# An audio layer on one core: joint index masks, a third index tile, and attention's output computed transposed

## The chip, the core and the metric

The kernel runs on one core of a Trainium2 chip. A core has five engines with queues of their own: PE (TensorE, matmuls from SBUF into PSUM; its weight loads are shown as PEld), DVE (VectorE), ACT (ScalarE), POOL (GpSimd) and SP (SyncE, which here issues every DMA). Each engine runs its own instructions in the order in which the program holds them, and waits where a semaphore says so. The metric is the device time of one execution in microseconds, lower being better.

## The reference

32 recordings of 160,000 samples are cut into S = 313 frames of 512 samples and transformed by a cosine basis. One layer follows: layer norm, attention with eight heads (softmax times a decay matrix, a group norm per head, a gate), a residual; then layer norm, a feed-forward part and a residual.

```python
h = einsum('bfh,kh->bfk', frames, D)
# attention, X = layernorm(h)
Q, K = xpos(X @ W_Q), xpos(X @ W_K, downscale)
p = softmax(Q @ K.T) * gamma ** abs(n - m)
Y = p @ V
Yn = (Yg - mu) * rsqrt(var + 1e-5)          # by head
h = h + (silu(X @ W_G) * (Yn * gn_weight + gn_bias)) @ W_O
# feed-forward, x = layernorm(h)
theta = x[..., None, :] / (1 + abs(W)) + B_param     # 256 units x 512 features
idx = mod(round(theta * 4096 / 2pi), 4096)
c, s = sum(cos_t[idx] * attn_cos, -1), sum(sin_t[idx] * attn_sin, -1)
h = h + silu(c @ proj_cos.T + s @ proj_sin.T)
```

The feed-forward part carries the bulk of the work: for each of 32 x 313 frames, 256 units and 512 features, one sine and one cosine.

## The kernel before, in words

**Feed-forward.** The 512 features lie as 4 groups of 128 partitions, frames along the free axis. Sequences go in pairs. A round handles 32 of the 256 units for the pairs that are resident just then (one to four of them, r = 2 to 8 sequences), so a pair stays for eight rounds; `STARTS` says in which of the 42 rounds each of the 16 pairs joins. There are 4 rounds of one pair, then 6 of two, 4 of three, 22 of four, and 2 each of three, two and one at the end. A round's work is cut into slots of at most 16 x 313 elements (two, four or eight combinations of a unit and a feature group; 12 x 313 elements with three pairs). For each slot:

- DVE writes table indices as int16 into a tile `ix` (L610, one instruction for each combination and run of neighbouring pairs), masks them in place (L622), writes a copy shifted by a quarter period into the next tile (L630) and masks that one in place (L636).
- ACT takes a sine of each of the two tiles into tiles `trig` (L643, "sines").
- PE multiplies each piece of `trig` by 32 columns of `hot`, which hold the attention weights of one unit in one column, and so adds up over features (L664, `pa` in PSUM). At the end of a round DVE copies the sums out (L681) and SP stores them.

Four `ix` tiles, three `trig` tiles, two `hot` tiles (one for each two units, 256 KB) and two tiles `f` (scale and offset of a round's units) rotate.

**Attention** of one sequence is laid between the slots. 313 rows are three blocks of 105 that overlap by one row. The buffers are in `Buffers`: three `ring` tiles through which all weights come, two `dec` tiles for decay matrices, `h`, `xn`, `xnT`, `prob`, `probT`, `u`, and four PSUM banks `W`. Two sequences are done before the first round (buffers A and B side by side), the other 30 with A during rounds. Its steps, in order: transform (`rows`, L273), layer norm (statistics L236, inverse root by `rsqrt`, normalisation L248), transposes (L260), values, and for each group of heads queries, keys and their rotated copies (`columns`, L288), the rotation in three DVE products (L341 to L346), scores (L355), maximum and difference (L363, L372), exponentials on ACT, row sums (L397), and for each head transposes (L412), the product with the decay (L424), the product with the values (L430: probabilities as stationary operand, result in rows) and the copy of it (L443). The group norm squares and sums (L467, L472 to L477), takes an inverse root, scales (L484), transposes back, and applies weight and bias (L494) and the gate (L499). `output` makes the last projection of a sequence (L531, L534).

`rsqrt` is two DVE instructions that make a seed (L215, L218) and twelve POOL instructions, three Newton steps of four (L224 to L227).

**What sets the order.** `Plan` takes every step with a key (its due place), an engine, an estimated duration, and what it reads and writes. `emit` runs a list schedule on these estimates: an engine that is free takes, of the steps whose predecessors have ended (plus `WAIT`, 400 ns, and for a load `LAND`, 3,500 ns), the one with the lowest key. The order found is the order in each engine's queue, SP's included. The estimates decide nothing else: on the chip an engine waits for what it really needs.

Of the kernel before, what the change touches and what calls it, by code (L numbers as in the profile page):

```python
# [21 lines left out]
P = 128  # L22
# [104 lines left out]
def tile_audio_tower(ctx: ExitStack, tc: tile.TileContext, t: dict, out: bass.AP):  # L127
# [7 lines left out]
    N_RING = 3  # L135
    N_IX, N_TRIG, N_HOT, N_PA = 4, 3, 2, 4
# [15 lines left out]
    class Buffers:  # L152


        def __init__(self, name, pool, psum):
            self.name = name
            self.n_ring = 0

# [4 lines left out]
            self.dec = [sb(f"dec{i}", STEP * (NT - 1) + S) for i in range(2)]  # L163

            self.u = sb("u", NC4, S)
            self.qk = [self.u[:, 2 * i : 2 * i + 2, :] for i in range(2)]
            self.h = sb("h", NT, HOP)
            self.v = self.h
            self.xn = sb("xn", NT, HOP)
            self.xnT = sb("xnT", NC4, S)  # L170
            self.prob = sb("prob", NB, NT, S)
            self.probT = sb("probT", NT, S)
            self.raw = self.probT[:, 0:2, :]
            wide = self.prob.rearrange("p a b s -> p (a b s)")
            self.sq = wide[:, : NT * HOP].rearrange("p (i d) -> p i d", d=HOP)
            self.hres = self.sq
            self.aff = wide[:, NT * HOP : NT * HOP + NC4 * S].rearrange("p (c s) -> p c s", s=S)
# [8 lines left out]

            self.y = self.W[:, 3, : NT * 2 * DH].rearrange("p (i d) -> p i d", d=2 * DH)
# [24 lines left out]
    def rsqrt(plan, key, val, r, u, kv, kr, ku):  # L212
# [17 lines left out]
        plan.add(key, "POOL", 3500, newton, (kv,), (kr, ku))  # L230

    def layernorm(plan, key, x):

        for i in range(NT):
            def stats(i=i):
                nc.vector.bn_stats(x.st[:N, i, :], x.h[:N, i, :])  # L236
                nc.vector.bn_aggr(x.mv[:N, i, :], x.st[:N, i, :])
            plan.add(key, "DVE", 850, stats, (x.k("h"),), (x.k("mv", i),))
# [6 lines left out]
        for i in range(NT):  # L245
            plan.add(
                key, "DVE", 490,
                lambda i=i: nc.vector.tensor_scalar(  # L248
                    x.xn[:N, i, :], x.h[:N, i, :], x.mv[:N, i, 0:1], x.lr[:N, i : i + 1],
                    ALU.subtract, ALU.mult,  # L250
                ),
                (x.k("h"), x.k("mv", i), x.k("lr")), (x.k("xn", i),),
            )

    def transposed(plan, key, x):

        for c in range(NC4):
            def go(c=c):
                for i in range(NT):
                    nc.tensor.transpose(  # L260
                        x.W[:, c, ROW0[i] : ROW0[i] + N], x.xn[:N, i, c * P : (c + 1) * P],
                        ident[:N, :N],
                    )
            plan.add(key, "PE", 800, go, x.every("xn", NT), x.banks(c))
# [28 lines left out]
    def attention(plan, keys, sq, x, eng):  # L293
# [9 lines left out]
        def residual(key, load):  # L303
            for i in range(NT):
                f0 = 1 if i and not load else 0
                d, s = h_d[sq, ROW0[i] + f0 : ROW0[i] + N, :], x.h[f0:N, i, :]
                kd, ks = ("h_d", sq), x.k("h")
                if load:
                    plan.add(key, "SP", DMA_NS, lambda d=d, s=s: nc.sync.dma_start(s, d), (kd,), (ks,))
                else:  # L310
                    plan.add(key, "SP", DMA_NS, lambda d=d, s=s: nc.sync.dma_start(d, s), (ks,), (kd,))

        xns, probs, us = x.every("xn", NT), x.every("prob", NB), x.every("u", 2)
# [3 lines left out]
        copy(plan, step(), eng, NT * HOP, x.h[:N], W3, x.banks(0, 1, 2), (x.k("h"),))  # L317
# [8 lines left out]
        copy(plan, step(), eng, NT * HOP, x.v[:N], W3, x.banks(0, 1, 2), (x.k("h"),))  # L326
        plan.add(step(0), "POOL", 500, lambda: nc.gpsimd.memset(x.v[0:1, : NT - 1, :], 0.0), (),
                 (x.k("h"),))

        for hb in range(H // NB):  # L330
            for g in range(hb * NB // 2, (hb + 1) * NB // 2):
# [8 lines left out]
                plan.add(key, "DVE", 810,  # L340
                         lambda qk=qk: nc.vector.tensor_tensor(qk, x.W[:, 0:2, :S], cos_qk, ALU.mult),  # L341
                         x.banks(0, 1), (kq,))

                def turned(qk=qk):
                    nc.vector.tensor_tensor(x.raw, x.W[:, 2:4, :S], sin_qk, ALU.mult)
                    nc.vector.tensor_tensor(qk, qk, x.raw, ALU.add)  # L346
                plan.add(key, "DVE", 1640, turned, x.banks(2, 3), (x.k("probT"), kq))
            for hd in range(hb * NB, (hb + 1) * NB):
# [16 lines left out]
                if a == NB - 1:  # L365
# [9 lines left out]
                         (x.k("mx", hd % 2), *x.banks(0, 1, 2)), (x.k("prob", a),))  # L375

            def exps(hb=hb, m=m):
                if eng == "DVE":
                    nc.scalar.activation(x.prob[:N, : NB - 1], x.prob[:N, : NB - 1], AF.Exp)
                for a in range(NB):  # L380
                    for i in range(NT):
                        last = a == NB - 1
                        if last or eng == "ACT":
                            nc.scalar.activation(  # L384
                                x.prob[:N, a, i, :],
                                x.W[:N, i, :S] if last else x.prob[:N, a, i, :], AF.Exp,
# [7 lines left out]
                     (x.k("mx", 1), *x.banks(0, 1, 2)), [*probs, x.k("sm", hb), x.k("lu")])  # L394
            for a in range(0, NB if eng == "DVE" else 0, 2):
                plan.add(step(0), "DVE", 2120,
                         lambda h0=hb * NB + a, a=a: nc.vector.tensor_reduce(  # L397
                             x.sm[:N, :, h0 : h0 + 2].rearrange("p i h -> p h i"),
                             x.prob[:N, a : a + 2], AX.X, ALU.add),
                         (x.k("prob", a), x.k("prob", a + 1)), (x.k("sm", hb),))  # L400
            for hd in range(hb * NB, (hb + 1) * NB):
                key = step(5)
                a, d = hd % NB, hd % 2
                plan.add(key, "SP", DMA_NS,
                         lambda hd=hd, d=d: nc.sync.dma_start(x.dec[d], t["decay"][hd]),
                         (), (x.k("dec", d),))
                for jj in range(NT):
                    j = NT - 1 - jj

                    def go(a=a, jj=jj, j=j):  # L410
                        for i in range(NT):
                            nc.tensor.transpose(  # L412
                                x.W[:N, jj, ROW0[i] : ROW0[i] + N],
                                x.prob[:N, a, i, ROW0[j] : ROW0[j] + N], ident[:N, :N],
                            )
                    plan.add(key, "PE", 800, go, (x.k("prob", a),), x.banks(jj))

                def decayed(d=d):
# [535 lines left out]
```

## Time and profile before

| What | us |
|---|---|
| median of three runs (18,890.79 to 18,904.49) | 18,893.47 |
| the profiled execution | 18,894.1 |
| its span, first to last instruction | 18,892.3 |
| ACT busy in sines, 4,288 of them (L643) | 17,547.6 |
| DVE busy in indices (L610), 5,888 instructions | 6,673.8 |
| DVE busy in L622, L630 and L636, 2,144 each | 3,023.7, 3,014.4, 3,017.3 |
| PE busy in the sine matmuls (L664), 131,072 | 10,373.1 |
| PE busy in the value products (L430), 4,464 for buffers A | 540.6 |
| POOL busy in all | 656.5 |

A busy time is a sum over one kind of instruction on one engine, and the engines work beside each other, so the rows do not add up to the span. PE's share says little by itself, since its matmuls are pipelined and their ends are modelled. What a row is worth is seen from the stage it lies in and from what the other engines wait for there.

### The profile page before, as it was taken

To read this page: it belongs to the slowest core of one execution; us is meant where nothing else is said; L and a number is where in the kernel's file an instruction comes from. 1 tells how busy PE (TensorE), PEld (TensorE's weight loads), DVE (VectorE), ACT (ScalarE), POOL (GpSimd) and SP (SyncE) were. 2 spreads that over 40 slices of the span, in tenths; PEclk is the share of its full clock that TensorE was granted. 3 is DMA by queue.
4 is the path that set the end of the run, shared out by engine and by line. 5 is a ranking of instruction groups with operands and counts; after the bars stand their busy time and mean duration, and the time that the engine had idled before them with its cause. 6 is when DMAs were issued, how large, how long until landed. Compare 5 with 4: busy or idle time off the path is not lost.

```text
span 18892.3 us, 332980 instructions
## 1 busy us (share of the span) xinstructions
PE 14803.3 (78%) x148864; PEld 6590.0 (35%) x148864; DVE 17770.2 (94%) x15244; ACT 18090.3 (96%) x5026; POOL 656.5 (3%) x1222
## 2 busy tenths in 40 slices
PE   8888888887888887888788888887888788766566
PEld 4433333333333333333333333333333333222222
DVE  5999999999999999999999999999999999889998
ACT  3899999999999999999999999999999999999998
POOL 0000000000000000000000000000000000000000
PEclk8999999999999999999999999999999999889998
DMA  3211111111111111111111111111111111000011
GB/s 96 66 52 48 50 57 47 46 51 47 31 35 37 46 42 41 32 40 46 38 45 39 32 44 41 45 40 36 39 38 46 39 45 35 24 10 25 12 30 46
DMA packets 447834, 783.69 MB, mean 41 GB/s; under 512 B 61601, under 2 KB 116129, under 8 KB 446401
## 3 DMA queue, kind: packets, MB, share of 16 engines
q1 hardware_dynamic: 446400, 762.39, 13.3%
q8 instruction: 1167, 19.12, 0.4%
q14 instruction: 267, 2.18, 0.0%
HBM read 657.51 MB, written 104.66 MB: 40 GB/s over the span
## 4 chain that ended last, share of the span: by engine, by line
DVE 55%; ACT 18%; PE 15%; issue 8%; POOL 3%; DMA 1%; DVEq 0%; SPq 0%; ACTq 0%; POOLq 0%
DVE ix L610 20%; ACT trig L643 18%; DVE ix L630 9%; DVE ix L622 9%; PE pa L664 8%; DVE ix L636 8%; PE a_W L288 3%; PE a_W L273 2%; DVE a_mx L363 1%; DVE a_prob L372 1%; DVE a_sm L397 1%; DVE a_probT L424 1%; DVE a_st L236 1%; PE a_W L355 1%; POOL a_lu L224 1%
## 5 line engine op out<-in xcount | busy, mean ns | idle before, releaser
L643 ACT ACTIVATE trig<-ix 128x5008 f32<-128x5008 int16 (+1 forms) x4288 | 17547.6, 4178 | 442.0 <-PE pa L664 185.5
L664 PE MATMUL pa<-trig,hot 128*32 128x313 f32 x131072 | 10373.1, 462 | 3021.0 <-ACT trig L643 3003.0
L664 PEld LDWEIGHTS pa<-trig,hot 128*32 128x32 f32 x131072 | 4058.5, 116 | 8907.0 <-ACT trig L643 4513.9
L610 DVE TENSOR_SCALAR ix<-xT,f 128x2504 int16<-128x2504 f32 (+3 forms) x5888 | 6673.8, 1184 | 211.9 <-ACT trig L643 205.8
L630 DVE TENSOR_SCALAR ix<-ix 128x5008 int16<-128x5008 int16 (+1 forms) x2144 | 3014.4, 1406 | 201.2 <-DVE ix L622 5.0
L622 DVE TENSOR_SCALAR ix<-ix 128x5008 int16<-128x5008 int16 (+1 forms) x2144 | 3023.7, 1410 | 69.2
L636 DVE TENSOR_SCALAR ix<-ix 128x5008 int16<-128x5008 int16 (+1 forms) x2144 | 3017.3, 1407 | 67.2
L288 PE MATMUL a_W<-a_xnT,a_ring 128*128 128x313 f32 x4960 | 1539.2, 446 | 220.1 <-DVE a_u L341 125.1
L273 PE MATMUL a_W<-a_ring,a_u 128*105 128x512 f32 x2256 | 1101.5, 623 | 120.8 <-DVE a_u L499 53.7
L288 PEld LDWEIGHTS a_W<-a_xnT,a_ring 128*128 128x128 f32 x4960 | 882.9, 191 | 868.2 <-issue 284.7
L430 PE MATMUL a_W<-a_h,a_probT 105*105 105x64 f32 x4464 | 540.6, 270 | 118.0 <-DVE a_probT L424 117.7
L273 PEld LDWEIGHTS a_W<-a_ring,a_u 128*105 128x105 f32 x2256 | 360.2, 174 | 722.8 <-issue 579.0
L430 PEld LDWEIGHTS a_W<-a_h,a_probT 105*105 105x105 f32 x4464 | 476.3, 181 | 386.4 <-issue 194.7
L355 PE MATMUL a_W<-a_u 64*105 64x313 f32 x1488 | 502.8, 466 | 112.0 <-DVE a_prob L372 100.6
L412 PE MATMUL a_W<-ident,a_prob 105*105 105x105 f32 x2232 | 325.9, 284 | 186.7 <-ACT a_prob L384 150.9
L273 PE MATMUL a_W<-a_ring,a_xnT 128*105 128x512 f32 x744 | 380.0, 631 | 50.9 <-DVE a_xnT L210 49.3
L224 POOL TENSOR_TENSOR a_gu<-a_gr 105x24 f32<-105x24 f32 x93 | 69.5, 747 | 10066.3 <-DVE a_gr L218 10061.4
L412 PEld LDWEIGHTS a_W<-ident,a_prob 105*105 105x105 f32 x2232 | 259.4, 185 | 344.9 <-ACT a_prob L384 193.2
L260 PE MATMUL a_W<-ident,a_xn 105*128 105x105 f32 x1116 | 190.2, 298 | 234.8 <-DVE a_xn L248 108.2
L355 PEld LDWEIGHTS a_W<-a_u 64*105 64x105 f32 x1488 | 239.3, 178 | 386.0 <-DVE a_prob L372 152.6
L363 DVE TENSOR_REDUCE a_mx<-a_W 105x3 f32<-105x939 f32 x248 | 280.2, 1130 | 17.7 <-PE a_W L355 17.1
L424 DVE TENSOR_TENSOR a_probT<-a_W,a_dec 105x939 f32<-105x939 f32 x248 | 279.9, 1129 | 13.0 <-PE a_W L412 13.0
(136 smaller groups left out, 3461.9 us busy)
## 6 DMA issues: line engine op xcount, KB each, us to landing
hot<-in_hot SPq DMA_DIRECT2D x672, 256.0 KB
a_dec<-in_decay SPq DMA_DIRECT2D x248, 260.5 KB
a_ring<-in_proj SPq DMA_DIRECT2D x128, 256.0 KB
a_ring<-in_dct SPq DMA_DIRECT2D x124, 256.0 KB
a_ring<-wv_d SPq DMA_DIRECT2D x124, 256.0 KB
a_ring<-in_wq SPq DMA_DIRECT2D x124, 256.0 KB
a_ring<-in_wk SPq DMA_DIRECT2D x124, 256.0 KB
a_ring<-in_wq_s SPq DMA_DIRECT2D x124, 256.0 KB
```

The costliest lines, as they stand in the source:

```text
L273: lambda c=c, i=i, k=k, to=to: nc.tensor.matmul(x.W[:N, to, :], lhsT[:, c, ROW0[i] : ROW0[i] + N], x.ring[k], start=(c == 0), stop=(c == N ...
L288: lambda c=c: nc.tensor.matmul(x.W[:, bank, :S], w[:, c, :], x.xnT[:, c, :], start=(c == 0), stop=(c == NC4 - 1)),
L355: lambda i=i, qk=qk, r0=r0: nc.tensor.matmul(x.W[:N, i, :S], qk[r0 : r0 + DH, 0, ROW0[i] : ROW0[i] + N], qk[r0 : r0 + DH, 1, :], start=Tru ...
L363: lambda m=m: nc.vector.tensor_reduce(m[:N], x.W[:N, :NT, :S], AX.X, ALU.max),
L412: nc.tensor.transpose(x.W[:N, jj, ROW0[i] : ROW0[i] + N], x.prob[:N, a, i, ROW0[j] : ROW0[j] + N], ident[:N, :N],)
L430: nc.tensor.matmul(x.y[:N, i, (hd % 2) * DH : (hd % 2 + 1) * DH], x.probT[:N, jj, ROW0[i] : ROW0[i] + N], x.v[:N, jj, hd * DH : (hd + 1) * ...
L610: nc.vector.tensor_scalar(now["ix", x][:, d0 : d0 + 2 * m * S], now["xT", c][:, 2 * at * S : 2 * (at + m) * S], f[:, 0, c, n + u : n + u + ...
L622: nc.vector.tensor_scalar(tl, tl, LUT - 1, LUT // 2, ALU.bitwise_and, ALU.bitwise_xor)
L630: nc.vector.tensor_scalar(tl[:, :E], now["ix", xs][:, :E], float(LUT // 4), None, ALU.add)
L636: nc.vector.tensor_scalar(tl, tl, LUT - 1, None, ALU.bitwise_and)
L643: nc.scalar.activation(tl[:, :E], now["ix", x][:, :E], AF.Sin, bias=-PI32, scale=ANG)
L664: nc.tensor.matmul(now["pa", p][g * 32 : g * 32 + 32, :S], now["hot", z][:, u, c, k, :], now["trig", w][:, s0 : s0 + S], start=(n == 0 and ...
```

## The change

- **Joint masks.** A tile `ix` now holds two halves. Indices go into the first half, one instruction writes the quarter-shifted copy into the second, and one instruction masks both. There are three such tiles in place of four single ones. Slots, sines and sine matmuls are as many as before.
- **Hot tiles** are cut in half (two units by two feature groups, 128 KB) and there are three of them. Tiles `f` go from two to one, `ring` from three to two, `dec` from two to one.
- **Values as stationary operand.** A value block of 105 x 64 is the weight, the transposed probabilities stream through, and the result comes out with features on partitions (`yT`). Heads are taken in the order 3, 2, 0, 1 of each four.
- **Group norm** on that layout: squares, sums over the 64 features of a head by matmuls with a matrix of ones (`of_head`), two fused instructions for the variance, the inverse root as before, three transposes of the 24 factors, a copy, and matmuls with `head_w`, which holds the weights, to spread the factors over the features; one product and four fused additions of the bias and products with the gate. The transposes back are gone.
- **The rotation** is one product over all four banks and one addition. Row sums are taken over one and over three heads instead of two and two. The layer norm writes its result over `h`; tile `xn` is gone.
- The planner's estimate for Newton's steps on POOL is 6,000 in place of 3,500, and estimates of the changed DVE steps are set anew.

```diff
-    N_RING = 3
-    N_IX, N_TRIG, N_HOT, N_PA = 4, 3, 2, 4
+    N_RING = 2
+    N_IX, N_TRIG, N_HOT, N_PA = 3, 3, 3, 4
...
-            self.dec = [sb(f"dec{i}", STEP * (NT - 1) + S) for i in range(2)]
+            self.dec = sb("dec", STEP * (NT - 1) + S)
...
-        plan.add(key, "POOL", 3500, newton, (kv,), (kr, ku))
+        plan.add(key, "POOL", 6000, newton, (kv,), (kr, ku))
...
-                for i in range(NT):
-                    def go(i=i, hd=hd):
-                        for jj in range(NT):
-                            nc.tensor.matmul(
-                                x.y[:N, i, (hd % 2) * DH : (hd % 2 + 1) * DH],
-                                x.probT[:N, jj, ROW0[i] : ROW0[i] + N],
-                                x.v[:N, jj, hd * DH : (hd + 1) * DH],
-                                start=(jj == 0), stop=(jj == NT - 1),
-                            )
-                    plan.add(key, "PE", 1000, go, (x.k("probT"), x.k("h")), x.banks(3))
+                e0 = hd % 2 * DH
+                for jj in range(NT):
+                    plan.add(
+                        key, "PE", 500,
+                        lambda jj=jj, hd=hd, e0=e0: nc.tensor.matmul(
+                            x.W[e0 : e0 + DH, 3, :S], x.v[:N, jj, hd // 2, e0 : e0 + DH],
+                            x.probT[:N, jj, :], start=(jj == 0), stop=(jj == NT - 1)),
+                        (x.k("probT"), hs[hd // 2]), x.banks(3))
...
+        def sums():
+            for i in range(NT):
+                for c in range(NC4):
+                    nc.tensor.matmul(x.W[:N, 0, i * H : (i + 1) * H],
+                                     x.sqT[:, c, ROW0[i] : ROW0[i] + N], of_head[:, c, :],
+                                     start=(c == 0), stop=(c == NC4 - 1))
+        plan.add(key, "PE", 2700, sums, probs, x.banks(0))
...
+            nc.vector.scalar_tensor_tensor(f(x.gv), f(x.sm), EPS, f(x.sm), ALU.mult, ALU.mult)
+            nc.vector.scalar_tensor_tensor(
+                f(x.gv), x.W[:N, 0, : NT * H], 1.0 / DH, f(x.gv), ALU.mult, ALU.add)
...
+        def factors():
+            for i in range(NT):
+                nc.tensor.transpose(x.W[:H, 1, ROW0[i] : ROW0[i] + N], x.gr[:N, i, :], ident[:N, :N])
+        plan.add(step(2), "PE", 700, factors, (x.k("gr"),), x.banks(1))
...
+        def spread():
+            for c in range(NC4):
+                nc.tensor.matmul(x.W[:, c, :S], head_w[:, c, :], x.rT, start=True, stop=True)
...
-                        def mask(x=x):
-                            tl = now["ix", x][:, :E]
-                            nc.vector.tensor_scalar(
-                                tl, tl, LUT - 1, LUT // 2, ALU.bitwise_and, ALU.bitwise_xor)
-                        plan.add(key, "DVE", 130 + 0.26 * E, mask, (), (("ix", x),))
...
-                        def quarter(x=x, xs=xs):
-                            tl = new("ix", x, [P, SLOT * S], I16, bufs=N_IX)
-                            nc.vector.tensor_scalar(
-                                tl[:, :E], now["ix", xs][:, :E], float(LUT // 4), None, ALU.add)
...
-                        def wrap(x=x):
-                            tl = now["ix", x][:, :E]
-                            nc.vector.tensor_scalar(tl, tl, LUT - 1, None, ALU.bitwise_and)
...
+            def quarter(x=x, E=E):
+                tl = now["ix", x]
+                nc.vector.tensor_scalar(tl[:, 1, :E], tl[:, 0, :E], float(LUT // 4), None, ALU.add)
+            plan.add(key, "DVE", 220 + 0.26 * E, quarter, (("ix", x, 0),), (("ix", x, 1),))
+
+            def mask(x=x, E=E):
+                tl = now["ix", x][:, :, :E]
+                nc.vector.tensor_scalar(
+                    tl, tl, LUT - 1, LUT // 2, ALU.bitwise_and, ALU.bitwise_xor)
+            plan.add(key, "DVE", 220 + 0.26 * 2 * E, mask, (), [("ix", x, i) for i in range(2)])
```

## The prediction

> **What bounds the kernel now.** I read the page's busy shares first, then busy time by stage, then the instruction groups by shape, then the waits, and last a timeline of one stall. The profiled execution took 18,894.1 us (span 18,892.3), 0.003% above the median of the runs shown, so sums made on it carry over.
>
> ```profile
> PE 14803.3 (78%) x148864; PEld 6590.0 (35%) x148864; DVE 17770.2 (94%) x15244; ACT 18090.3 (96%) x5026; POOL 656.5 (3%) x1222
> ```
>
> ScalarE is idle for 802 us in all, so a change that leaves its work alone can win no more than that. The columns of the next view are window, length, then busy us and (instructions) of PE, PEld, DVE, ACT, POOL.
>
> ```profile
> 0.00:331.00 331.00, 279.13 (x1088) 181.54 (x1088) 137.92 (x186) 52.60 (x122) 17.77 (x82) 0.85 0.37 115
> 331.00:1020.00 689.00, 559.10 (x5051) 282.33 (x5052) 647.79 (x852) 593.84 (x246) 37.59 (x76) 0.89 0.22 66
> 1020.00:2840.00 1820.00, 1481.63 (x14401) 689.85 (x14403) 1743.48 (x1688) 1705.04 (x490) 82.43 (x152) 0.93 0.17 51
> 2840.00:4690.00 1850.00, 1490.20 (x14578) 673.65 (x14574) 1763.55 (x1654) 1730.82 (x577) 77.78 (x152) 0.96 0.15 47
> 4690.00:16060.00 11370.00, 9176.72 (x92958) 4075.45 (x92950) 10878.04 (x8237) 11243.61 (x2879) 440.89 (x760) 0.93 0.13 40
> 16060.00:18892.00 2832.00, 1816.48 (x20812) 687.14 (x20804) 2599.46 (x2632) 2764.43 (x716) 0.00 (x0) 0.91 0.08 24
> ```
>
> Length minus ACT's column gives ACT's idle time: 278 us before the first sine, then 95, 115 and 119 in the rounds of one, two and three pairs ("early", 329 in 4,359 us), 126 in the wide rounds with attention, 68 at the end. Early, VectorE is the busier engine (4,155 against 4,030); wide, ScalarE is (98.9%). So DVE work taken out counts early, and little later.
>
> ```profile
> ACT trig L643 <- PE pa L664: 52.2, 25, 3.8
> ACT trig L643 <- DVE ix L636: 29.9, 29, 2.5
> ACT a_xn L531 <- PE a_W L273: 20.2, 9, 3.8
> ...
> ACT trig L643 <- DVE ix L622: 7.0, 11, 3.9
> ```
>
> These are ACT's waits in the wide rounds (4,690 to 16,060; total us, times, longest): only 37 of its 126 idle us are charged to DVE.
>
> **The joint mask.** Of a slot's five or more DVE instructions it removes one: mask, quarter and wrap become a quarter and one mask over both halves.
>
> ```profile
> L622 DVE TENSOR_SCALAR ix<-ix 128x5008 int16<-128x5008 int16 x1760 | 2586.2, 1469 | 57.5
> L622 DVE TENSOR_SCALAR ix<-ix 128x3756 int16<-128x3756 int16 x384 | 437.6, 1139 | 11.7
> ```
>
> The two shapes give (1,469 - 1,139) / 1,252 = 0.26 ns an element and a fixed part near 0.166 us (all three lines agree within 5 ns). The elements stay, so each slot saves one fixed part: 2,144 slots x 0.166 = 356 us of DVE, of which 512 slots (64 + 192 + 256) lie early: **85 us**. [...] A gap of some 31 ns before the dropped instruction (69.2 us over 2,144) may go too: 0 to 16 us early, taken as 8. Where three pairs run, the joint mask is a pattern of 2 x 3,756, a shape the trace lacks. Its bounds are 2.1 us (this rate) and 4.1 us (half of it); I take the first, because element type and step are those of the row.
>
> **Attention on DVE, per sequence**: the rotation, four times 0.804 + 0.806 + 0.812, becomes 1.46 (a 1,252-element row) + 0.812, -0.6; four output copies at 0.551 become 0.478 (the 128x313 copy from PSUM), -0.3; squares 1.755 to 1.46, -0.3; variance 1.747 + 0.293 + 0.183 + 0.183 + 0.178 becomes two of 0.18, -2.2; the 1.758 scaling becomes a 0.478 copy and a 1.46 product, +0.2; the affine part, 4 x 0.596 + 1.46, becomes four fused ones whose price lies between 0.478 and 0.596, taken as 0.55, -1.6. Row sums keep their elements. Sum -4.9 us; ten sequences finish early: **49 us**. ScalarE loses only five squares of about 0.3 us.
>
> **PE** nets nothing. 144 narrow y matmuls, 540.6 / 31 = 17.4 us a sequence, become 48 wide ones at 0.31 (1,539 / 4,960), 14.9. Twelve transposes go (2.0); 24 tiny matmuls with ones (0.121 each, 2.9), three transposes (0.5) and 8 spreading matmuls (2.5) come: +1.4 us.
>
> **Newton on POOL** is planned at 6.0 us instead of 3.5, so DVE is given more work before it asks for the result. Now it waits 2.4 us each time (below: total, times, longest), 67 us of this early, with the 2.3 us waits at L484.
>
> ```profile
> DVE a_xn L248 <- POOL a_lr L227: 150.4, 62, 3.3
> ```
>
> Would the longer plan remove that? Here is one such stall.
>
> ```profile
> 7484.79 1.39 POOL L224 TENSOR_TENSOR a_lu<-a_lr 105x3 f32<-105x3 f32 x1 [77.72 <-DVE a_lr L218]
> 7486.26 1.42 POOL L225 TENSOR_TENSOR a_lu<-a_lu,a_lv 105x3 f32<-105x3 f32 x1
> 7487.76 1.41 POOL L226 TENSOR_SCALAR a_lu<-a_lu 105x3 f32<-105x3 f32 x1
> 7489.26 0.19 POOL L227 TENSOR_TENSOR a_lr<-a_lr,a_lu 105x3 f32<-105x3 f32 x1
> ```
> ```profile
> 7484.55 3.07 DVE L610 TENSOR_SCALAR ix<-xT,f 128x2504 int16<-128x2504 f32 x2
> 7487.66 1.47 DVE L622 TENSOR_SCALAR ix<-ix 128x5008 int16<-128x5008 int16 x1
> 7491.69 1.46 DVE L248 TENSOR_SCALAR a_xn<-a_h,a_mv,a_lr 105x512 f32<-105x512 f32 x3 [2.57 <-POOL a_lr L227]
> ```
>
> Three POOL operations end just after three DVE instructions; once DVE stands still they take 0.19 us, one every 0.275. [...] By the plan's figure alone all 67 us would go. [...] Net **9 us**. [...]
>
> **Loads.** Ring buffers go from 3 to 2, decay from 2 to 1, the scale table f from 2 to 1, hot tiles from two whole to three halves. These loads now wait for a nearer reader: f for the last index of its round, decay for the previous head's product, hot for PE two halves back. A sums load landed 2.1 us after its issue, and f is covered by the 4.2 us of quarter and mask, so 0 if SP is free; if SP, which issues in order, stands at a hot load, DVE waits up to 3 us a round, 14 early rounds, 0 to 42. I take 5. In one-pair rounds a slot needs two of the three hot halves; freeing one, issue and landing (0.4 + 2.1) and the 2.3 us run that follows make about 5 us, under the slot's 8.56, so 0, and 64 early slots x 1 us if a load is held. Before the first sine the two sequences alternate on PE (279 of 331 us busy): cheaper y, a longer group-norm chain and thinner rings: -15 to +15, taken as 0. The last two outputs reload two ring tiles late, +3; the 32 last slots of one pair give 5 back.
>
> **Sum.** Early DVE: 85 + 8 + 49 + 9 - 5 = 146, leaving DVE at 4,213 against ACT's 4,030, so still the bound; I let nine tenths through, 131, since part of ACT's early idle time (58.1 + 29.7 + 39.9 = 128 us) is charged to PE, which gains nothing. Wide: a third joint index tile lets DVE run three slots ahead instead of two and its load falls; the 37 us go. End: 2. Total 170: 18,894 - 170 = 18,724, **forecast 18,720**, own range 18,650 to 18,800.
>
> **Rivals.**
> - *Everything couples* (0.2): early ACT idles only as in the wide rounds, 1.1% of 4,359 = 47, so 282 go, and with it half of the wide 126: 18,550. For it: ACT's own early work allows it. Against: the DVE sum has only 146.
> - *PE takes the wait* (0.14): the 128 us charged to PE stay and the thinner loads eat the wide gain; 60 are won: 18,830. For it: attention's bursts of 10.5 us on PE block sines now. Against: DVE never starved for it long.
> - *The factors block PE* (0.05), the slower side: group-norm factors reach PE only when POOL is done. [...] Three sine tiles cover 3 x 4.28 less two runs of 2.3, 8.2 us. From there each microsecond is ACT's. If PE stands 15 us, 7 x 30 = 210 are lost and 170 won: 18,935.
> - *The joint mask doesn't do what it says* (0.01): at half rate 2.5 us a slot, DVE bound throughout: above 20,000.
>
> The forecast keeps 0.6. The range reaches to both near rivals and the bounds of loads and start: 18,560 to 18,850. Under 0.2% (38 us) a measurement of this kernel would not tell a change. Faster 0.87: forecast, coupling and most of the PE case; same 0.07; slower 0.06.
>
> **What would show it.** A joint mask at 2.77 us and 2.1; DVE busy down by about 510 us and ACT unchanged; the early stages shorter by some 130 us, ending near 4,560; waits of the normalisation on POOL at 1.6 us instead of 2.4; no new wait on f or hot. I am wrong if the early end hardly moves, if ACT's waits on PE grow around the factors, or if the wide rounds gain more than 60.

## The result and the profile after

The changed kernel takes 18,708.7 us (median of 4 runs, 18,703.5 to 18,713.1) where the kernel before takes 18,895.2 on the same chip: a ratio of 0.9900 (95% interval 0.9886 to 0.9914). That is 186 us less, against 170 to 174 forecast. The profiled execution has a span of 18,701.4 us, 191 less than before.

The sum came out nearly right, its parts did not. The stages, cut at the sines that begin them, show it; the last two columns are ACT's idle time.

| Stage | before, us | after, us | difference | expected | idle before | idle after |
|---|---|---|---|---|---|---|
| before the first sine | 331.0 | 356.8 | +26 | 0 | 278 | 304 |
| rounds of one pair | 697.3 | 705.3 | +8 | about -20 | 98 | 106 |
| rounds of two pairs | 1,828.7 | 1,778.7 | -50 | about -55 | 113 | 66 |
| rounds of three pairs | 1,837.7 | 1,779.3 | -58 | about -55 | 119 | 64 |
| rounds of four pairs ("wide") | 12,476.2 | 12,363.1 | -113 | -37 | 134 | 29 |
| the rest | 1,721.4 | 1,718.2 | -3 | -2 | 60 | 61 |

("About" is the forecast's 131 us of the early stages, spread over them.) The first line of the changed kernel's page, the busy time by engine, stands against the one shown of before:

```profile
PE 14815.8 (79%) x146528; PEld 6384.0 (34%) x146528; DVE 17294.6 (92%) x12876; ACT 18071.2 (97%) x5026; POOL 1038.5 (6%) x1190
```

DVE has lost 476 us of work, ACT 19, and POOL is busy 1.6 times as long with fewer instructions. By window (columns as before: window, length, then busy us and instructions of PE, PEld, DVE, ACT, POOL):

```profile
356.80:1062.20 705.40, 582.87 (x4939) 275.46 (x4940) 633.74 (x781) 599.06 (x248) 51.93 (x74) 0.89 0.22 65
1062.20:2840.90 1778.70, 1494.17 (x14196) 670.88 (x14199) 1707.86 (x1476) 1712.94 (x492) 136.75 (x148) 0.93 0.18 53
2840.90:4620.20 1779.30, 1483.35 (x14224) 648.86 (x14217) 1700.05 (x1363) 1715.55 (x576) 141.87 (x148) 0.95 0.16 48
4620.20:16983.20 12363.00, 9900.25 (x99725) 4222.56 (x99723) 11546.06 (x7351) 12333.62 (x3136) 689.54 (x740) 0.93 0.13 38
```

With two and three pairs ACT is now a little busier than DVE, where it was the other way round: DVE no longer bounds these stages by its work. With one pair DVE is busier still, and DVE stands idle for 72 and ACT for 106 of 705 us, so something else holds them. In the wide rounds ACT is busy for 99.8% of the window. Its waits there, from 4,625 us on (total us, times, longest; the stage's first wait, 7.4 us for the joint mask, lies before):

```profile
ACT trig L651 <- DVE ix L643: 14.1, 10, 3.0
ACT trig L651 <- PE pa L673: 5.8, 8, 0.9
ACT trig L651 <- issue: 4.9, 2, 2.5
ACT a_h L550 <- PE a_W L278: 1.8, 1, 1.8
```

(L651 is the sines, L643 the joint mask, L673 the sine matmuls, L278 the row products, L550 the output's activation.) Not only the waits charged to DVE are gone, as forecast: of those charged to PE, 54.0 us in the sines and 25.9 in the output over the whole wide stage, 7.6 are left. That is the second thing to explain; the first is the beginning, where 34 us were lost and 20 should have been won.

### The profile page after: what moved, and what is told of

Its sections match the earlier page's. It is cut to its first block, busy times and chain, and to the rows that moved or that the text cites. A ratio compares the mean times of both kernels' runs of the same rounds, so it can differ in the third digit from the quotient of the medians.

```text
span 18701.4 us, 327934 instructions
## 1 busy us (share of the span) xinstructions
PE 14815.8 (79%) x146528; PEld 6384.0 (34%) x146528; DVE 17294.6 (92%) x12876; ACT 18071.2 (97%) x5026; POOL 1038.5 (6%) x1190
## 2 busy tenths in 40 slices
DMA packets 716481, 783.43 MB, mean 42 GB/s; under 512 B 72344, under 2 KB 470936, under 8 KB 715072
## 3 DMA queue, kind: packets, MB, share of 16 engines
q1 hardware_dynamic: 715072, 762.46, 13.6%
## 5 line engine op out<-in xcount | busy, mean ns | idle before, releaser
L651 ACT ACTIVATE trig<-ix 128x5008 f32<-128x5008 int16 (+1 forms) x4288 | 17531.7, 4177 | 278.3 <-PE pa L673 143.3
L673 PE MATMUL pa<-trig,hot 128*32 128x313 f32 x131072 | 10330.4, 460 | 3243.6 <-ACT trig L651 3184.5
L673 PEld LDWEIGHTS pa<-trig,hot 128*32 128x32 f32 x131072 | 4053.3, 115 | 9223.5 <-ACT trig L651 4911.7
L626 DVE TENSOR_SCALAR ix<-xT,f 128x2504 int16<-128x2504 f32 (+3 forms) x5888 | 6657.8, 1182 | 87.9 <-DMA xT<-xT_d 62.5
L643 DVE TENSOR_SCALAR ix<-ix 128x10016 int16<-128x10016 int16 (+1 forms) x2144 | 5686.4, 2652 | 65.0
L638 DVE TENSOR_SCALAR ix<-ix 128x5008 int16<-128x5008 int16 (+1 forms) x2144 | 3028.7, 1413 | 633.8 <-ACT trig L651 479.6
L278 PE MATMUL a_W<-a_ring,a_u 128*105 128x512 f32 x2256 | 1098.8, 620 | 73.7 <-DMA a_u<-in_frames 23.9
L229 POOL TENSOR_TENSOR a_gu<-a_gr 105x24 f32<-105x24 f32 x93 | 101.5, 1092 | 9975.8 <-DVE a_gr L223 9776.0
L278 PEld LDWEIGHTS a_W<-a_ring,a_u 128*105 128x105 f32 x2256 | 358.1, 174 | 674.6 <-issue 618.4
L445 PE MATMUL a_W<-a_probT,a_h 105*64 105x313 f32 x1488 | 494.1, 464 | 43.6 <-DVE a_probT L438 43.4
L278 PE MATMUL a_W<-a_ring,a_xnT 128*105 128x512 f32 x744 | 367.1, 619 | 11.4 <-DVE a_xnT L215 9.9
L229 POOL TENSOR_TENSOR a_lu<-a_lr 105x3 f32<-105x3 f32 x186 | 149.2, 802 | 3587.4 <-DVE a_lr L223 3577.6
L445 PEld LDWEIGHTS a_W<-a_probT,a_h 105*64 105x64 f32 x1488 | 192.8, 147 | 358.5 <-issue 159.1
L426 PE MATMUL a_W<-ident,a_prob 105*105 105x105 f32 x1674 | 244.8, 275 | 11.4 <-DVE a_h L455 11.3
L426 PEld LDWEIGHTS a_W<-ident,a_prob 105*105 105x105 f32 x1674 | 183.5, 172 | 187.8 <-issue 158.6
L347 DVE TENSOR_TENSOR a_prob<-a_W,turn_qk 128x1252 f32<-128x1252 f32 x124 | 180.4, 1454 | 66.7 <-issue 35.2
```

Source lines behind the costliest of these rows:

```text
L278: lambda c=c, i=i, k=k, to=to: nc.tensor.matmul(x.W[:N, to, :], lhsT[:, c, ROW0[i] : ROW0[i] + N], x.ring[k], start=(c == 0), stop=(c == N ...
L426: nc.tensor.transpose(x.W[:N, jj, ROW0[i] : ROW0[i] + N], x.exp[a][:N, i, ROW0[j] : ROW0[j] + N], ident[:N, :N],)
L445: lambda jj=jj, hd=hd, e0=e0: nc.tensor.matmul(x.W[e0 : e0 + DH, 3, :S], x.v[:N, jj, hd // 2, e0 : e0 + DH], x.probT[:N, jj, :], start=(jj ...
L626: nc.vector.tensor_scalar(now["ix", x][:, 0, d0 : d0 + 2 * m * S], now["xT", c][:, 2 * at * S : 2 * (at + m) * S], f[:, 0, c, n : n + 1], ...
L638: nc.vector.tensor_scalar(tl[:, 1, :E], tl[:, 0, :E], float(LUT // 4), None, ALU.add)
L643: nc.vector.tensor_scalar(tl, tl, LUT - 1, LUT // 2, ALU.bitwise_and, ALU.bitwise_xor)
```

## Experiments

Each run is set against the kernel before on its own chip (18,899.6 to 18,903.4 us there), and the differences, not the times, are compared across chips. An edit is to the changed kernel where nothing else is said, and "..." stands for lines left out. Totals are medians; stages and waits come from one profiled execution of each run, which can lie off the median (with two index tiles it took 18,842.0 us, 14 above).

**Two index tiles in place of three** (the mask stays joint).

```diff
-    N_IX, N_TRIG, N_HOT, N_PA = 3, 3, 3, 4
+    N_IX, N_TRIG, N_HOT, N_PA = 2, 3, 3, 4
```

> The changed kernel with two joint index tiles instead of three, all else kept (the plan's order is made anew). The wide rounds lost 105 us of ScalarE idle time with the change, where I had counted on 37. Theory 1 (run-ahead): the third tile did it, letting VectorE stand three slots ahead, so that waits of the group norm and of the layer norm no longer reach ScalarE; then ScalarE's idle time in the wide rounds goes back from 29 us to 80 or more, and the whole takes 18,770 to 18,810. Theory 2 (load): VectorE's smaller load and the new plan did it, and two tiles, which hold as many slots as the four single ones did, are enough: 18,710 to 18,730, wide idle time below 50.

**Two masks in place of one** (three tiles stay): each half is masked by an instruction of its own.

```diff
+            def mask(x=x, E=E):
+                tl = now["ix", x][:, 0, :E]
+                nc.vector.tensor_scalar(
+                    tl, tl, LUT - 1, LUT // 2, ALU.bitwise_and, ALU.bitwise_xor)
+            plan.add(key, "DVE", 220 + 0.26 * E, mask, (), [("ix", x, 0)])
...
-            def mask(x=x, E=E):
-                tl = now["ix", x][:, :, :E]
-                nc.vector.tensor_scalar(
-                    tl, tl, LUT - 1, LUT // 2, ALU.bitwise_and, ALU.bitwise_xor)
-            plan.add(key, "DVE", 220 + 0.26 * 2 * E, mask, (), [("ix", x, i) for i in range(2)])
+            def wrap(x=x, E=E):
+                tl = now["ix", x][:, 1, :E]
+                nc.vector.tensor_scalar(tl, tl, LUT - 1, None, ALU.bitwise_and)
+            plan.add(key, "DVE", 220 + 0.26 * E, wrap, (), [("ix", x, 1)])
```

> The changed kernel with three instructions a slot again: mask of the first half, quarter copy, mask of the second half; three two-half tiles kept. By the price of the joint mask (0.166 us a slot, and up to 0.03 of gap) the early stages, bound by VectorE, get longer by 85 to 100 us (512 slots). Wide rounds: if VectorE's load set ScalarE's idle time there (theory 2), it grows by 40 us or more and the whole takes about 18,840; if the third tile did (theory 1), the wide rounds stay within 15 us and the whole takes about 18,800.

**Both at once**, which leaves attention's rewrite, the thinner loads and the planner's estimate.

> Edit: both parts of the change on indices undone, e1 and e2 together (two tiles of two halves, which is the room of the four single tiles before, and two masks): what stays is attention's rewrite, the thinner loads and the planner's estimate. Theory (the index part carries all of the gain; attention's saving of DVE time, some 49 us on the early sequences, is eaten by the start, the hot loads and the estimate, which lost 44 us in e7): the losses of e1 and e2 add up, 18,890 to 18,925, no faster than the kernel before. Rival (the losses of e1 and e2 overlap, and attention's part carries its 49 us and more): 18,835 to 18,870.

The three runs and the change make a square (median; in brackets the ratio to before and its interval):

| | two masks | one joint mask |
|---|---|---|
| two tiles | 18,861.5, 42 less than before [0.9969, 0.9988] | 18,827.5, 75 less [0.9947, 0.9977] |
| three tiles | 18,793.0, 109 less [0.9927, 0.9957] | 18,708.7, 186 less [0.9886, 0.9914] |

So the third tile is worth 67 us with two masks and 112 with the joint one, the joint mask 33 us with two tiles and 77 with three. Together they bring 145 of the 186, and about 45 of these only when both are there. The intervals are 18 to 28 us to either side, and those of the two runs with two tiles overlap, so the 45 is a rough size; but no run of one of the four kernels came within 14 us of a run of another. For the run with both undone the rival's range held (18,835 to 18,870), and my theory that the index part carries everything fell: what stays, attention's part with the loads and the planner's figure, is worth 42 us net. Its stages of two and three pairs, 1,808.0 and 1,811.7 us, are 47 shorter than before, its wide rounds 29, while its start and its one-pair rounds are longer by 24 and 11.

In the wide rounds, 12,447.4 us with both undone, the third tile alone gives 12,381.7 and the joint mask alone 12,472.0. The joint mask alone gains nothing there: it loses 25 us, of which some 19 may be the executions profiled (14 above the median here, 5 below it with both undone), but the other run with two joint tiles, below, has 12,484.9. Its waits say why:

```profile
ACT trig L651 <- DVE ix L643: 76.6, 62, 3.6
ACT trig L651 <- PE pa L673: 41.2, 48, 4.1
```

These are ACT's wide waits with the joint mask and two tiles. Both sines of a slot now wait for one 2.77 us instruction at the end of the slot's DVE work, where before the first went off while the quarter copy was still being written; with both undone the sines wait 38.0 us for the two masks. With two tiles DVE seems not to be far enough ahead to hide that, and with three the row is down to 14.1. Of my two theories for the two-tile run, the one that puts the gain on the third tile held in kind (ACT's idle time in the wide rounds went back to 124 us) and was too low in time (18,770 to 18,810). The run with two masks bore it out as well: its wide rounds are 19 us longer, and it took 18,793.

**The planner's figure for Newton's steps**, back to 3,500 in the changed kernel, and alone at 6,000 in the kernel before.

```diff
-        plan.add(key, "POOL", 6000, newton, (kv,), (kr, ku))
+        plan.add(key, "POOL", 3500, newton, (kv,), (kr, ku))
```

> The changed kernel with the old estimate of 3.5 us for Newton's steps. [...] The rival, that the longer estimate is what keeps PE from standing at the factors with sine matmuls behind them, expects ScalarE's waits on PE in the wide rounds to go from 6 us back to 50 or more: 18,760 to 18,800.

> Edit: the kernel before, with the planner's estimate for Newton's steps at 6,000 in place of 3,500 and nothing else. [...] Rival (the estimate is what shortens the early stages): 18,840 to 18,870, with the stages of two and three pairs 15 to 25 us shorter each.

In the changed kernel the figure is worth nothing: 18,710.5 us [0.9883, 0.9916], 192 less than before; I had expected 18,720 to 18,750, the rival 18,760 to 18,800, and both fell. The waits of the normalisation on POOL are 115.2 us there and 101.5 with 6,000, where I had expected about 150. In the old kernel the figure costs 44 us: 18,946.1 [1.0013, 1.0031]. I had expected next to no effect (18,885 to 18,910), and the rival a gain of 30 to 60; both fell. Yet the waits it was to shorten did shrink, to the 100 to 130 us expected. DVE's waits of the normalisation on POOL, in the old kernel and in the old kernel with 6,000:

```profile
DVE a_xn L248 <- POOL a_lr L227: 150.4, 62, 3.3
```
```profile
DVE a_xn L248 <- POOL a_lr L227: 108.6, 59, 2.0
```

42 us of DVE's waiting were taken away and the kernel became longer. ACT's waits on the first mask rose from 126.8 to 144.2 us, its waits in the output (L531) from 71.9 to 98.1, the first sine came 11.4 us later, and the wide rounds grew by 33. The figure moves the order of everything behind it, and the new order cost more than the waits gave back.

**The start.** The timeline suggested that, in the changed kernel, the last normalisation of sequence A (319.2 us) stands in DVE's queue behind B's addition, statistics and seed, though its factors were ready at 313.8, and that the chain of the third sequence (frames, transform, statistics) and with it the first index hang on that. I tried a third ring tile before the rounds, the order, and both.

```diff
-            i = self.n_ring % N_RING
+            i = self.n_ring % self.n_bufs
...
+    early = inner.enter_context(tc.tile_pool(name="early_ring", bufs=1))
+    for x in (A, B):
+        x.ring.append(early.tile([P, HOP], F32, name=f"{x.name}_ring2"))
+        x.n_bufs = 3
...
+    A.n_ring, A.n_bufs = 0, N_RING
...
```

> The changed kernel with a third ring buffer for each of the two sequences before the first sine alone (it lies where the rounds' tiles come later). The first sine came 26 us later with the change, where I had said 0. Theory: with two ring buffers the row products of A and B alternate in pieces, so A ends later and its layer norm starts later; the transposes of the last layer norm are 13 us later for this than the group norm explains. Then the first sine comes 10 to 16 us earlier, at 341 to 347, and the whole takes 18,690 to 18,700. Rival: the longer chain of the group norm explains all 26 us; then the first sine stays at 355 to 358 and the whole at 18,709.

```diff
-                 x.banks(0, 1, 2), hs)
+                 (*x.banks(0, 1, 2), *(A.rows_of if x.name == "b" else ())), hs)
```

> Edit: only before the rounds, the residual addition of sequence B (L521) is planned behind the last normalisation of sequence A (L253), so that A's normalisation no longer stands behind B's addition, statistics and seed in DVE's queue. Theory (the start is lengthened by this order: A's normalisation at 319.2 us holds up A's transposes, the store of xT, the frames load of the third sequence, its transform and its statistics, which stand ahead of the first index on DVE): A's normalisation starts near 313.9, all that follows moves forward by about 5 us, the first sine falls from 356.9 to 351 to 353, and the time by about 5 us, to 18,700 to 18,706. Rival (B's chain sets the start, and A's place is harmless): first sine 357 to 360, time unchanged or 1 to 3 us longer.

> Edit: the order of e5 together with a third ring tile for A and B before the rounds only (as in e4). Theory (both were given up by the change and either alone is not enough: with two ring tiles the row products of A and B alternate on PE, and A ends late; with three, A is ready at 311.4 us but waits in DVE's queue to 318.5): A's normalisation at about 311.5, first sine at 348 to 351, time 5 to 9 us below the changed kernel, about 18,700. Rival (B's chain sets the start): first sine 356 to 360, no gain.

First sines at 357.0, 358.4 and 355.5 us, against 356.8; times 18,704.2, 18,715.2 and 18,711.1 us. All three ideas fell: on their own chips these are 198, 187 and 191 us less than before. With the order alone A's normalisation did come at 313.6, but what followed went against B. Part of the timeline of that run (start, length, engine, line, operation; in brackets the idle time before and what ended it):

```profile
326.13 5.06 PE L278 MATMUL a_W<-a_ring,a_u 128*105 128x512 f32 x8 [9.92 <-DMA a_u<-in_frames]
326.67 0.55 DVE L253 TENSOR_SCALAR b_h<-b_h,b_mv,b_lr 105x512 f32<-105x512 f32 x1 [2.39 <-DMA h_d<-b_h]
...
331.03 1.25 PE L265 MATMUL b_W<-ident,b_h 105*128 105x105 f32 x12
```

The third sequence's transform (L278), now ready earlier, goes ahead of B's transposes (L265) on PE and holds them for 5 us. B's normalisation waits 2.4 us for a store: it writes over `h` since the tile `xn` is gone, so the residual has to be stored first. The first sine needs both sequences.

**Loads of hot.** SP issues every load in order. Its own waits in the one-pair rounds (total us, times, longest; L616 loads hot, L207 ring tiles, L419 decay):

```profile
SPq L616 <- PE pa L673: 290.3, 105, 19.6
SPq L207 <- PE a_W L293: 86.3, 39, 5.2
SPq L419 <- DVE a_probT L438: 73.5, 16, 12.4
```

The window is 357 to 1,040. For 290 of these 683 us SP stands at a load of hot, with attention's loads behind it. The first test gave the room of the third index tile to a fourth half hot tile and a second tile `f`, and is compared with the two-tile run above.

> Edit: as e1 (two joint index tiles), and the room of the third is given to a fourth half hot tile and a second tile f. To be compared with e1 (18,827.5; one-pair rounds 706.4 us). Theory (loads of hot and f cost under 5 us in all, and the 8 us by which the one-pair rounds grew come from attention's work on PE): 18,817 to 18,832, one-pair rounds 702 to 707, the same waits of ACT on PE. Rival (the thinner loads are what the one-pair rounds lost and part of what the early stages lack): one-pair rounds 685 to 698, early stages 20 to 40 us shorter, 18,785 to 18,810.

One-pair rounds 681.1 us in place of 706.4: the rival was right there, my "under 5 us" wrong. The whole gained little by the medians (18,821.5 us, 81 less than before against 75), which is my range and not the rival's. In the executions profiled it is 24 us shorter, with wide rounds 13 us longer; the two-tile one lay 14 above its median, so what took the gain back is not settled. Then with three index tiles, room made in two ways:

```diff
-    N_IX, N_TRIG, N_HOT, N_PA = 3, 3, 3, 4
+    N_IX, N_TRIG, N_HOT, N_PA = 3, 3, 4, 4
...
-                    u = place("part", 2)
+                    u = place("part", 1)
...
```

> Edit: the changed kernel (three joint index tiles, one tile f) with a fourth half hot tile; the room comes from the second of the two tiles 'part' through which a round's sums are stored. Theory (in e8 it was the hot tiles: SP, which issues in order, stands 290 us of the one-pair rounds at loads of hot, with ring and decay loads of attention behind it, and PE waits 8 us for hot): one-pair rounds 680 to 690 us in place of 705, other stages as before, 18,685 to 18,698 in all. Rival (in e8 it was the second tile f, or the freer order of its loads): one-pair rounds 702 to 708, no gain; and where the single tile part is too few, the wide rounds grow by 5 to 30 us.

```diff
-    N_IX, N_TRIG, N_HOT, N_PA = 3, 3, 3, 4
+    N_IX, N_TRIG, N_HOT, N_PA = 3, 3, 6, 4
...
-                             new("hot", z, [P, 2, 2, 2, 32], bufs=N_HOT),
-                             t["hot"][:, blk * UNITS + n : blk * UNITS + n + 2, c : c + 2]),
+                             new("hot", z, [P, 2, 1, 2, 32], bufs=N_HOT),
+                             t["hot"][:, blk * UNITS + n : blk * UNITS + n + 2, c : c + 1]),
...
```

> Edit: the changed kernel with hot tiles cut once more, six tiles of two units by one feature group (64 KB) in place of three of two groups: the same bytes and the same room, twice as many loads of half the size. Theory (what a load of hot waits for is the last sine matmul on its tile; a quarter is free earlier, and SP stands less): one-pair rounds 690 to 700 us, 18,690 to 18,705 in all. Rival (room, not grain, is what counts, and SP has 1,344 more issues of about 0.4 us and DMA packets of half the size): one-pair rounds 703 to 715, 18,705 to 18,740.

Quarters (18,717.4 us, 182 less than before; one-pair rounds 714.2) win nothing: it is room that counts, not grain. The fourth half shortened the one-pair rounds to 689.9 us, but the kernel took 18,834.1, with wide rounds of 12,483.6. I had allowed 5 to 30 us for the single tile `part`; it cost 120. PE's waits in these wide rounds name it (L691 copies a round's sums to `part`):

```profile
PE pa L673 <- ACT trig L651: 2079.0, 1643, 6.1
PE pa L673 <- DVE part L691: 110.4, 33, 6.5
```

DVE can't copy the second bank before the first is stored, the next round's matmuls wait for the bank, and ACT for them: 133.8 us in 35 waits. So the last edit lets one tile serve as the second `part` while two or more pairs are resident and as the fourth half of hot while one is.

```diff
+    def hot_place(r):
+        if r == 2:
+            used["turn"] = used.get("turn", -1) + 1
+            if used["turn"] % (N_HOT + 1) == N_HOT:
+                return ("swap", 0)
+        return ("hot", place("hot", N_HOT))
...
-                    u = place("part", 2)
+                    used["parts"] = used.get("parts", -1) + 1
+                    u = ("swap", 0) if r > 2 and used["parts"] % 2 else ("part", 0)
...
```

> Edit: the changed kernel with one of its two tiles 'part' kept as a tile that is a fourth half of hot while one pair is resident, and the second tile 'part' while two or more are. Theory (hot loads cost the one-pair rounds 15 to 25 us, as e8 and e9 have it, and what e9 lost in the wide rounds came from the single tile part): one-pair rounds 680 to 692 us in place of 705, the last rounds of one pair 277 to 282 in place of 289, the wide rounds within 10 us of the changed kernel's 12,363, and 18,675 to 18,695 in all, 15 to 35 below the changed kernel. Rival (the gain in the one-pair rounds is given back later, since the time is set elsewhere, or the wide rounds' loss in e9 came from the order and not from part): 18,705 to 18,830.

18,693.4 us (18,684.4 to 18,695.8), 210 less than before, ratio 0.9888 [0.9873, 0.9903]. One-pair rounds 690.5 us, the last rounds of one pair 277.2 in place of 289.0, wide 12,372.1. The stages moved where the theory said, by 15 and 12 us, and SP's waits with them (the load of hot is L630 in this kernel):

```profile
SPq L630 <- PE pa L686: 223.1, 99, 19.2
SPq L419 <- DVE a_probT L438: 112.3, 16, 19.2
SPq L207 <- PE a_W L293: 91.8, 39, 5.6
```

SP stands 67 us less at hot and 39 more at the single decay tile: the queue has found its next narrow place. This is the fastest version tried. That it beats the changed kernel rests on the two stages, for the two intervals overlap, and the two executions profiled differ by 8 us only: the rounds of three and four pairs are 4 and 9 us longer in it, the start 2.

## Why the prediction was right, and where its steps were not

**The joint mask** was priced right for one instruction and too high for the stage. It takes 2.77 and 2.12 us, as forecast, the shape of 2 x 3,756 included.

```profile
L643 DVE TENSOR_SCALAR ix<-ix 128x10016 int16<-128x10016 int16 x1760 | 4873.8, 2769 | 53.2
L643 DVE TENSOR_SCALAR ix<-ix 128x7512 int16<-128x7512 int16 x384 | 812.6, 2116 | 11.8
```

Quarter and joint mask are busy 8,715 us where the three lines before had 9,055: 340 us less, against 356, or 0.159 us a slot. The row's 0.166 was near it. Undone alone, the early rounds grow by 62 us (6, 25 and 31), not by the 85 + 8 of the sum: "nine tenths through" should have been two thirds.

The step that failed is "4,213 against ACT's 4,030, so still the bound". The 4,213 is a length with DVE's own idle time in it, the 4,030 is busy time. Busy against busy, 4,155 less the 85 and 49 makes 4,021, under ACT's 4,030. Measured are 4,042 for DVE and 4,028 for ACT (the first three windows above), and the three stages lost 100 us in place of 131. So DVE's lead over ACT was used up on the way, with two and three pairs altogether, and what DVE saves beyond that need not shorten a stage.

**Attention on DVE**, -4.9 us a sequence: by the busy times 476 - 340 - 16 (indices) = 120 us, or 3.7 for each of 32. The eight sequences of the two- and three-pair rounds were to bring 39 us there; with both index parts undone these rounds are 47 shorter. So the step held in kind, but the 47 is more than the 30 us of DVE work saved there, and no run has attention's rewrite without the new loads and the planner's figure. The two sequences with one pair brought nothing; the loads, below, can account for it.

**Newton, +9 us.** No run shows this term, which was an estimate of mine; in its place the runs show a planner's figure worth 0 us in the changed kernel and -44 in the old one. The waits did get shorter. A stall of the changed kernel, DVE and POOL side by side:

```profile
7499.15 1.47 DVE L638 TENSOR_SCALAR ix<-ix 128x5008 int16<-128x5008 int16 x1
7500.65 2.77 DVE L643 TENSOR_SCALAR ix<-ix 128x10016 int16<-128x10016 int16 x1
...
7509.72 1.46 DVE L253 TENSOR_SCALAR a_h<-a_h,a_mv,a_lr 105x512 f32<-105x512 f32 x3 [1.75 <-POOL a_lr L232]
```
```profile
7499.17 1.49 POOL L230 TENSOR_TENSOR a_lu<-a_lu,a_lv 105x3 f32<-105x3 f32 x1
7500.75 2.72 POOL L231 TENSOR_SCALAR a_lu<-a_lu 105x3 f32<-105x3 f32 x1
...
7508.11 0.20 POOL L231 TENSOR_SCALAR a_lu<-a_lu 105x3 f32<-105x3 f32 x1
```

In this stall each POOL operation beside a DVE instruction is about as long as that: 2.72 us beside the joint mask's 2.77, 1.41 to 1.49 beside the others' 1.47 to 1.58. Once DVE stands still they take 0.19 or 0.20 us, one every 0.275. Six are done between seed and use, six are left, and DVE waits 1.75 us; six times 0.275 is 1.65. Over the whole run the wait is 1.7 us, with 1.6 forecast and 2.4 before:

```profile
DVE a_h L253 <- POOL a_lr L232: 101.5, 59, 2.6
```

In the early rounds these waits fell from 41.2 to 20.7 us, but those for the group norm's factors rose from 25.9 to 41.6, so 5 us net were won in place of 9. And I put the shorter waits into the sum as time, which those two runs do not bear out. A wait of DVE is only worth its length if the new order is otherwise as good.

**Loads, -5 us, 0 for hot with one pair.** This step failed in size and in place. I had the load of hot hidden under a slot of 8.56 us, named 64 slots x 1 us as a bound and took 0. That SP might stand at it I had seen, but I counted only DVE's wait for `f`. SP does stand, and attention's ring and decay loads stand behind it. The fourth half returns 15 us early and 12 at the end. The named sign, "no new wait on f or hot", was wrong: PE waits 8.2 us for hot with one pair. A wait not on my list, DVE on loads of `xT`, came to 62.5 us: 40.5 in the wide rounds, where DVE has 817 us to spare, and 22.0 before them, 14.0 of these where the second pair joins.

**The wide rounds, 37 us.** They gained 113, and by the prediction's own sign (more than 60) I was wrong there. I counted only the waits charged to DVE, gave them all to the third tile, and put attention's part at nothing here. The runs divide the 113: 29 us come with both index parts undone (12,447.4), the third tile brings 66 more (12,381.7), and the joint mask on top of it 19. With the joint mask in place the third tile is worth 109 (12,472.0 without it).

The waits on PE go the same way. In the sines they are 54.0 us before, 30.5 with both index parts undone, 15.4 with the third tile alone, 41.2 with the joint mask alone and 5.8 with both. A higher clock of PE is not the reason: in the fastest version the mean granted clock of the run is 0.925, where it was 0.926 before, and 7.2 us of such waits are left. Along which chain a tile of DVE's relieves PE was not traced.

**The start, 0 (-15 to +15).** It took +26, outside my bounds. In the old kernel the planner's figure alone goes with a first sine 11.4 us later. In the changed one neither that figure, nor a ring tile, nor A's place returns anything. The output's row products begin at 285.0 us in place of 274.9, so 10 us are lost before the last projection, where the group norm's chain now runs through POOL, PE, DVE and PE; but with the figure alone the old kernel begins them at 283.2. PE's granted clock may have a share too, which the prediction left out. From 278.1 to 295.2 us, when PE spreads the factors and begins the output, the changed kernel's granted clock is 0.50; in the old kernel it is 1.00 from 277.6 to 301.5, where most of its row products run. Over the whole start (columns as before, then the granted clock):

```profile
0.00:356.80 356.80, 288.84 (x942) 161.77 (x942) 129.96 (x170) 52.47 (x122) 18.43 (x80) 0.84 0.34 105
```

To three digits the granted clock is 0.842 in these 356.8 us and 0.847 in the 331.0 of before. What is missing to 1 makes 56 and 51 us, so by this estimate the clock can have added 6 us at most. No run tells whether the clock made the start late or the new order lowered the clock. How the 26 us divide between order, chain and clock stays open.

**The rivals.** *Everything couples* did not come: 236 us of early idle time remain, not 47. *PE takes the wait* has some truth with one pair, where the sines' waits on PE grew from 58 to 75 us, but not beyond. *The factors block PE*: PE does stand for the group norm's factors, 3.7 us on average and 6.3 at the longest,

```profile
PE a_W L497 <- POOL a_gr L232: 111.1, 30, 6.3
```

which is under the 8.2 us that three sine tiles were to cover, and in the wide rounds, with 20 of these 30 stands, only 5.8 us of waiting on PE reach ACT.

The total of 170 was near the 191 of the executions profiled because two errors of opposite sign met: 76 us too little in the wide rounds, and 57 too much at the start and in the early stages. That the sum came out so near is luck; that the early rounds win by DVE's work is not, as the run with two masks shows.

## What to carry to other kernels

Deeper buffering and fewer instructions are not added up: here the third tile was worth 67 us alone and 112 with the joint mask, which was worth 33 alone and 77 with the tile, and the waits that a buffer removes are not only those charged to the engine that fills it. When tiles are thinned, read the waits of the queue that issues the loads, in the stage where each load is used fastest; what stands behind the waiting load pays, here 15 us of the one-pair rounds. A planner's estimate is an edit of the whole order: it can shorten the wait it was meant for and lengthen the kernel, here by 42 and 44 us. And a length, waits included, is not to be set against another engine's busy time when the question is which of the two bounds a stage.

## What the runs showed of the hardware

POOL's busy time rose from 656.5 to 1,038.5 us with 32 instructions fewer. Two edits go with it. With the planner's figure more of its small operations lie beside DVE instructions (six of twelve in the stall above, three in the one shown of before): alone it raises the old kernel's 656.5 to 835.8, and taken back it lowers the changed kernel's 1,038.5 to 855.5. And the joint mask is a longer instruction to stand beside (2.72 us for POOL's operation there, 1.49 beside the quarter copy): 977.0 with it in place of 896.5 with two tiles, 1,038.5 in place of 944.4 with three.

A matmul with eight rows of weights took about as long as one of full height (0.30 us against 0.31), and its length went with PE's granted clock. The eight that spread the factors, in the start of the changed kernel and in a round of one pair:

```profile
278.30 4.54 PE L504 MATMUL a_W<-a_prob,head_w 8*128 8x313 f32 x8 [0.85 <-DVE a_prob L500]
663.90 2.37 PE L504 MATMUL a_W<-a_prob,head_w 8*128 8x313 f32 x8
```

The granted clock is 0.50 in the first case and 1.00 in the second, that is 0.57 and 0.30 us each, and the sum had taken 0.31 from a row of full height (1,539 / 4,960). Of the 32 groups of eight, 22 took 2.37 us, at a granted clock of 0.99 or 1.00, and eight took 4.53 or 4.54, at 0.50; over all rounds the mean is 89.2 / 248 = 0.36 us each.

DMA packets rose from 447,834 to 716,481 with 783 MB moved in both kernels. The main queue's packets took 13.3% of the DMA engines' time before and 13.6% after, so the smaller pieces show next to no price in bandwidth here.
